# A token router: ranks by full comparison and one-hot products, against a threshold searched by its bits and rows moved by indirect DMA

## The chip, the cores and the metric

The kernel runs on one core of a Trainium2 chip. The core has a matrix engine (TensorE, PE in the profile; its weight loads are the row PEld), a vector engine (VectorE, DVE), an activation engine (ScalarE, ACT), a general engine (GpSimd, POOL) and a queue engine (SyncE, SP) that only issues DMAs here. Each engine works through its own list of instructions in order and waits on semaphores. The metric is device time in microseconds for one execution, the median over runs.

## The reference

One sequence of 2048 tokens with 128 features passes through two layers. Each layer computes `x + s * silu(f)`, where `s` is an attention of the normalised input and `f` a second branch.

- First layer, `s`: attention with 16 heads of 8 features over all 2048 tokens, with relu in place of softmax; then an output product and a layer norm.
- First layer, `f`: a block for a few tokens. A router gives each token a weight (`x @ router_w + b`). The 255 tokens with the greatest weights are fetched in order of their place in the sequence, pass through a causal softmax attention with rotary positions and a small feed-forward part, are multiplied by their weight, and are put back at their places. All tokens whose weight is not above the 256th greatest keep `x`:

```
topv, topi = jax.lax.top_k(weights, k)          # k = 256
thr = topv[:, -1]
sel_mask = (weights > thr[:, None])
sel_idx = jnp.sort(topi[:, :kc], axis=1)        # kc = 255
...
out = jnp.zeros_like(x).at[bidx, sel_idx].set(proc)
return out + x * (1.0 - sel_mask)[..., None]
```

- Second layer: causal softmax attention with 16 heads of 64 features and a gated feed-forward part.

The selection must be exact: which tokens are among the 255, the threshold, and the places.

## The kernel before

**The loop.** `relu_attention` (L680) holds the first layer's attention as a loop of 256 steps (L964), n = 16 * (4 * qc + g) + kb, over 4 blocks of 512 queries, 4 groups of 4 heads and 16 blocks of 128 keys. A step issues four score products (`scores`, L824) into banks of PSUM, four evictions with relu (on ACT, L832, or on DVE, L834), and the four products with the values of the step two before (`products`, L840). Score banks are six, evicted tiles twelve, so engines may run about a step apart. In some steps a projection for later keys or queries stands behind them (`all_keys`, `all_queries`: `spread`, L728 on PE, L733 on ACT, L734 on DVE, then DMAs L738); in all other steps one turn of a generator of side work (`next(other)`, L976).

**The side work.** `others` (L950) runs `routed_block` (L217), then loads weights of the second layer, then `gated` (L863) for each block of queries that is ready. A `yield` ends a turn, so a piece of side work that is written between two `yield`s falls into one step of the loop. PE, ACT and DVE run exactly in the order in which the program is written (`manual_schedule`, L88); the lists of SP and POOL are arranged by the framework. Which of ACT and DVE takes an eviction is decided by `Work.lesser` (L189): it holds a running sum of planned work for each, to which side work adds its own with `work.add`, and gives the eviction to the one with the lesser sum.

**The router before.** PE forms the weights of all tokens as a row repeated in all partitions (`wrow`, 128 x 2048, L281) and as columns (`wcol`, 128 x 16, L289). The rank of every token is then counted on DVE: for each of 16 blocks of 128 tokens one comparison with all earlier tokens (L303), one with all others (L310) and one inside the block that settles ties (L314). For each pair of blocks two one-hot matrices 128 x 256 (`hot`, L331: is the token's rank equal to the column's number) are multiplied on PE with the rows `xne` (131 columns: 128 features, weight, place, position; L341), and the results are summed in `xs` on DVE (L346). The 256th row gives the threshold through a product with a mask of the last row (`last`, L353). So the fetched rows stand in order of weight; the block's own causal mask is fetched by their places (`mcols`, L366, and `msel`, L417, the two indirect DMAs of this kernel, on POOL).

**The way back before** (L632 to L677). For each block of 512 tokens DVE makes two one-hot matrices 128 x 512 (`place`, L642), PE multiplies them with the block's result `proc` (L652, 8 products of 128 columns), DVE adds the tokens that keep `x` (`unsel`, L658), ACT applies silu, and POOL folds in the bias, gamma and beta (L663 to L674). The blocks follow each other two or three steps apart.

**Around it.** At the start POOL makes constants (`tok`, `before`, `last`, L245 to L257), and clears `qk` and `v` (L268, L270), while DVE normalises the first tokens (`normalised`, L764 to L787, with L776 and the short chain L779 to L783). SP loads keys and queries of later groups back from DRAM (`group`, L742) between the DMAs of the side work.

Of the kernel before, what the change touches and what calls it, by code (L numbers as in the profile page):

```python
# [11 lines left out]
F32 = mybir.dt.float32  # L12
F32R = mybir.dt.float32r
BF16 = mybir.dt.bfloat16
I32 = mybir.dt.int32
U32 = mybir.dt.uint32
AF = mybir.ActivationFunctionType
ALU = mybir.AluOpType
AX = mybir.AxisListType
# [3 lines left out]
P = 128  # L23
S = 2048
D = 128
NC = S // P
NQ = S // 512
# [3 lines left out]
KSEL = 256  # L31
KC = KSEL - 1
SM = 512
NP = 8
NHB = 3
NS = 6
NEG = -1.0e30
MAGIC = 1.5 * 2.0**23

# [177 lines left out]
def routed_block(  # L217
# [3 lines left out]
    nc = tc.nc  # L221
    scale = 1.0 / math.sqrt(HD0)
    KB = (P, KC - P)

    def bank(shape):
        return ps.tile(shape, F32, tag="x", name="x")
# [3 lines left out]
    for t, n in enumerate(("wq", "wk", "wv")):  # L230
# [10 lines left out]
    nc.sync.dma_start(out=pos, in_=a["pos"])  # L241


    tok = rb.tile([P, 512], F32, name="tok")
    nc.gpsimd.iota(  # L245
        tok, pattern=[[1, 512]], base=0, channel_multiplier=0,
        allow_small_or_imprecise_dtypes=True,
    )
    before = rb.tile([P, P], F32, name="before")
    nc.gpsimd.memset(before, 1.0)  # L250
    nc.gpsimd.affine_select(
        out=before, in_=before, pattern=[[-1, P]], compare_op=ALU.is_gt,
        fill=0.0, base=0, channel_multiplier=1,
    )
    last = rb.tile([P, P], F32, name="last")
    nc.gpsimd.memset(last, 1.0)
    nc.gpsimd.affine_select(  # L257
        out=last, in_=last, pattern=[[0, P]], compare_op=ALU.is_ge,
        fill=0.0, base=-(P - 1), channel_multiplier=1,
    )  # L260
    nc.gpsimd.iota(
        xne[:, :, 129], pattern=[[P, NC]], base=0, channel_multiplier=1,
        allow_small_or_imprecise_dtypes=True,
# [11 lines left out]
    wrow = rb.tile([P, S], F32, tag="wrow_qkT", name="wrow")  # L275
    wcol = rb.tile([P, NC], F32, name="wcol")
    for i in range(NQ + 1):
        if i < NQ:
            cols = slice(512 * i, 512 * i + 512)
            t = bank([P, 512])  # L280
# [4 lines left out]
        if i:  # L285
            t = bank([P, 4, P])
            for c4 in range(4):
                c = 4 * i - 4 + c4
# [3 lines left out]
            yield  # L292
    nc.gpsimd.tensor_copy(xne[:, :, 128], wcol)


    junk = rb.tile([P, S], BF16, tag="junk_mrows", name="junk")
    cnt = rb.tile([P, 3, NC], F32, name="cnt")
    nc.vector.memset(cnt, 0.0)
    for c in range(NC):
        w = wcol[:, c : c + 1]  # L300
        lo = c * P
        if c:
            nc.vector.tensor_scalar(  # L303
                junk[:, :lo], wrow[:, :lo], w, None, ALU.is_ge, ALU.add,
                accum_out=cnt[:, 0, c : c + 1],
            )
            if c >= NC // 2:
                work.add(d=0.2 + lo / 960)
                yield
        nc.vector.tensor_scalar(  # L310
            junk[:, lo:], wrow[:, lo:], w, None, ALU.is_gt, ALU.add,
            accum_out=cnt[:, 1, c : c + 1],
        )
        nc.vector.scalar_tensor_tensor(  # L314
            junk[:, :P], wrow[:, lo : lo + P], w, before, ALU.is_equal, ALU.mult,
            accum_out=cnt[:, 2, c : c + 1],
        )
        work.add(d=2.9 if c < NC // 2 else 2.7 - lo / 960)
        yield
    rank = rb.tile([P, NC], F32, name="rank")  # L320
    nc.vector.tensor_reduce(rank, cnt.rearrange("p a c -> p c a"), AX.X, ALU.add)


    xs = rb.tile([P, 2, 131], F32, name="xs")
    made = []
    for c in range(-2, NC, 2):
        hots = made
        if c + 2 < NC:
            made = [rw.tile([P, KSEL], F32, tag="og", bufs=4, name="hot") for _ in range(2)]
            for i in range(2):  # L330
                nc.vector.tensor_scalar(  # L331
                    made[i], tok[:, :KSEL], rank[:, c + 2 + i : c + 3 + i], None, ALU.is_equal
                )
            work.add(d=0.7)
        if c < 0:
            yield
            continue
        t = bank([P, 2, 131])
        for b in range(2):
            for i in range(2):  # L340
                nc.tensor.matmul(  # L341
                    t[:, b, :], hots[i][:, b * P : (b + 1) * P], xne[:, c + i, 0:131],
                    start=(i == 0), stop=(i == 1),
                )
        if c:
            nc.vector.tensor_tensor(xs, xs, t, ALU.add)  # L346
        else:
            nc.vector.tensor_copy(xs, t)
        work.add(d=0.5)
        yield  # L350
    thr = small.tile([P, 1], F32, tag="thr")
    t = bank([P, 1])
    nc.tensor.matmul(t, last, xs[:, 1, 128:129], start=True, stop=True)  # L353
    nc.vector.tensor_copy(thr, t)
    unsel = rb.tile([P, NC], F32, name="unsel")
    nc.vector.tensor_scalar(unsel, wcol, thr, None, ALU.is_le)

# [49 lines left out]
    for b in range(2):  # L407
        t = bank([P, 4, P])
# [113 lines left out]
    for g in range(G):  # L522
# [28 lines left out]
        prT = []  # L551
# [78 lines left out]


    b_out, gamma, beta, xin = rest  # L632
    at = small.tile([P, 2, NQ], F32, tag="at")
    for i in range(NQ):
        nc.gpsimd.tensor_scalar(at[:, :, i], xs[:, :, 129], 512.0 * i, None, ALU.subtract)
    for i in range(NQ + 1):
        if i:
            put = place
        if i < NQ:
            place = [rw.tile([P, 512], F32, tag="prT", bufs=4, name=f"place{b}") for b in range(2)]  # L640
            for b in range(2):
                nc.vector.tensor_scalar(place[b], tok, at[:, b, i : i + 1], None, ALU.is_equal)  # L642
            work.add(d=1.0)
            yield
        if not i:
            continue
        cs = slice(4 * i - 4, 4 * i)
        t = bank([P, 4, D])
        for c4 in range(4):
            for b in range(2):  # L650
                n = KB[b]
                nc.tensor.matmul(  # L652
                    t[:, c4, :], put[b][:n, c4 * P : (c4 + 1) * P], proc[:n, b, :],
                    start=(b == 0), stop=(b == 1),
                )
        for c4 in range(4):
            c = 4 * i - 4 + c4
            nc.vector.scalar_tensor_tensor(  # L658
                g0[:, c, :], xne[:, c, 0:D], unsel[:, c : c + 1], t[:, c4, :],
                ALU.mult, ALU.add,  # L660
            )
        work.add(d=1.4)
        nc.gpsimd.tensor_tensor(  # L663
            xne[:, cs, 0:D], xne[:, cs, 0:D], b_out.unsqueeze(1).to_broadcast([P, 4, D]), ALU.add
        )
        yield
        nc.scalar.activation(g0[:, cs, :], g0[:, cs, :], AF.Silu)
        work.add(a=0.7)
        u = rw.tile([P, 4, D], F32, tag="qkv", name="gb")
        nc.gpsimd.tensor_tensor(  # L670
            u, g0[:, cs, :], beta.unsqueeze(1).to_broadcast([P, 4, D]), ALU.mult
        )
        nc.gpsimd.tensor_tensor(xin[:, cs, :], xin[:, cs, :], u, ALU.add)
        nc.gpsimd.tensor_tensor(  # L674
            g0[:, cs, :], g0[:, cs, :], gamma.unsqueeze(1).to_broadcast([P, 4, D]), ALU.mult
        )
        yield  # L677


def relu_attention(  # L680
# [1045 lines left out]
```

## Time and profile before

| | |
|---|---|
| median of 3 runs | 1487.89 us (1487.07 to 1488.57) |
| the profiled execution: its time | 1487.12 us |
| the profiled execution: its span, first to last instruction | 1485.1 us |
| mean granted clock of TensorE | 0.991 |
| DMA | 44.70 MB, mean 30 GB/s |
| loop of the first layer, first scores to last products | 37.7 to about 505 us |

The page gives the busy time of each engine, then the span in 40 equal slices (37.1 us each) with the busy share of a slice in tenths. A group of instructions is told by line, engine, operation and tile. A matmul's end is modelled, so TensorE can look busy while it waits; the distance between the starts of like instructions is the safer measure. A matmul of two fp32 operands is recorded as two instructions.

### The profile page before, as it was taken

The page shows a single profiled execution, that of the slowest core. Times are in us where ns is not written, and L with a number is a line of the kernel's source. Part 1 is how long each engine was busy: PE and PEld are TensorE (multiplying, and loading weights), DVE is VectorE, ACT ScalarE, POOL GpSimd, SP SyncE. Part 2 cuts the span into 40 slices and gives each one's busy share as a digit, 9 for nine tenths or more (in the row PEclk, how much of TensorE's full clock was granted, in tenths as well). Part 3 has the DMA queues.
Part 4 walks back from the last instruction along what each step waited for, and adds up shares of the span by engine and source line. Part 5 has one row for each costly group of instructions (what it writes and reads, how often), then busy time and mean ns, then how long its engine had stood idle before and what let it go on. Part 6 is the DMA issues. An engine that isn't in the chain of part 4 may idle for free.

```text
span 1485.1 us, 27124 instructions
## 1 busy us (share of the span) xinstructions
PE 1431.8 (96%) x10336; PEld 877.3 (59%) x10336; DVE 1079.6 (73%) x1938; ACT 967.2 (65%) x2080; POOL 325.2 (22%) x445
## 2 busy tenths in 40 slices
PE   4999999999999999999999999999999999999997
PEld 2223233332222367777777777777777777777775
DVE  5797878778888667567677667667767766777765
ACT  2787878778878656656556556556656655665663
POOL 1001000050000123322332242242242232252310
PEclk8999999999999999999999999999999999999999
DMA  2621100100200220000010010010001001000000
GB/s 66 186 66 61 32 12 14 49 26 14 60 20 4 79 50 15 15 16 15 21 24 15 15 30 15 15 29 15 15 15 29 15 15 29 15 15 16 15 22 22
DMA packets 28192, 44.70 MB, mean 30 GB/s; under 512 B 5984, under 2 KB 14560, under 8 KB 28064
## 3 DMA queue, kind: packets, MB, share of 16 engines
q1 hardware_dynamic: 27376, 41.94, 11.0%
q8 instruction: 81, 1.33, 0.4%
q0 software_dynamic: 256, 0.79, 0.2%
q14 instruction: 47, 0.39, 0.1%
q10 hardware_dynamic: 432, 0.26, 0.1%
HBM read 14.76 MB, written 10.11 MB: 17 GB/s over the span
## 4 chain that ended last, share of the span: by engine, by line
PE 60%; ACT 2%; DVE 1%; issue 1%; DVEq 0%; ACTq 0%
PE t L1326 18%; PE z L1376 17%; PE t L1556 16%; PE m L1436 2%; PE m L1264 2%; PE m L1229 2%; PE m L1279 2%; PE m L1421 2%; ACT p L1360 1%; ACT pt L1563 1%; PE m L1158 0%; DVE tops L1347 0%; PE m L1176 0%; DVE t L1346 0%; DVE pt L1563 0%
## 5 line engine op out<-in xcount | busy, mean ns | idle before, releaser
L1347 DVE TENSOR_REDUCE tops<-t 128x1 f32<-128x1024 f32 (+4 forms) x320 | 334.6, 1062 | 63.2 <-PE t L1326 56.0
L832 ACT ACTIVATE rt<-t 128x512 f32<-128x512 f32 x620 | 326.3, 625 | 76.1 <-PE t L824 75.0
L1563 ACT COPY pt<-t 128x512 f32<-128x512 f32 (+3 forms) x359 | 163.4, 518 | 266.9 <-PE t L1556 265.8
L1360 ACT ACTIVATE p<-t,tops 128x1024 f32<-128x1024 f32 (+7 forms) x384 | 331.2, 882 | 2.9 <-DVE tops L1347 2.2
L1326 PE MATMUL t<-k,q 128*128 128x512 f32 (+4 forms) x1280 | 316.6, 390 | 7.4 <-ACT p L1360 7.4
L834 DVE TENSOR_SCALAR rt<-t 128x512 f32<-128x512 f32 x404 | 261.2, 684 | 45.4 <-PE t L824 38.6
L840 PE MATMUL t<-rt,va 128*9 128x512 f32 x2048 | 270.3, 601 | 4.2 <-ACT part L856 3.8
L1556 PE MATMUL t<-ident,p 128*128 128x128 f32 x2176 | 270.1, 275 | 3.0 <-ACT x L1250 1.4
L1376 PE MATMUL z<-pt,v 128*64 128x256 f32 (+1 forms) x2304 | 268.3, 374 | 0.5 <-ACT zs L1570 0.5
L1326 PEld LDWEIGHTS t<-k,q 128*128 128x128 f32 x1280 | 218.6, 189 | 79.7 <-issue 36.1
L1556 PEld LDWEIGHTS t<-ident,p 128*128 128x128 f32 x2176 | 244.0, 141 | 25.5 <-ACT pt L1563 2.9
L1376 PEld LDWEIGHTS z<-pt,v 128*64 128x64 f32 x2304 | 151.6, 136 | 86.9 <-issue 21.4
L824 PEld LDWEIGHTS t<-qT,kT 32*128 32x128 f32 x1024 | 64.8, 183 | 189.0 <-ACT rt L832 112.9
L1563 DVE COPY pt<-t 128x512 f32<-128x512 f32 (+3 forms) x289 | 163.5, 605 | 2.6 <-PE z L1376 1.5
L824 PE MATMUL t<-qT,kT 32*128 32x512 f32 x1024 | 157.3, 500 | 4.5 <-DVE rt L834 3.1
L1346 DVE TENSOR_TENSOR t<-t,mask_q 128x128 f32<-128x128 f32 (+1 forms) x192 | 65.0, 339 | 85.8 <-PE t L1326 78.3
L1252 POOL CAST q<-x 64x512 fp32r<-64x512 f32 x60 | 36.8, 613 | 371.7 <-ACT x L1250 338.9
L1360 ACT ACTIVATION_READ_ACCUMULATOR p<-t,tops 128x1 f32 x384 | 84.1, 219 | 0.0
L1426 DVE TENSOR_TENSOR zs<-zs,m 128x512 f32<-128x512 f32 (+1 forms) x49 | 32.7, 676 | 64.3 <-PE m L1421 64.1
L1254 POOL TENSOR_TENSOR k<-x,k 64x512 fp32r<-64x512 f32 x60 | 76.4, 1273 | 4.6
L1254 POOL TENSOR_TENSOR q<-x,q 64x512 fp32r<-64x512 f32 x60 | 76.3, 1272 | 4.6
L840 PEld LDWEIGHTS t<-rt,va 128*9 128x9 f32 x2048 | 30.7, 88 | 69.5 <-issue 61.0
(291 smaller groups left out, 1068.1 us busy)
## 6 DMA issues: line engine op xcount, KB each, us to landing
q<-q SPq DMA_DIRECT2D x64, 256.0 KB
spread<-high SPq DMA_DIRECT2D x16, 256.0 KB
spread<-low SPq DMA_DIRECT2D x16, 256.0 KB
qT<-spread SPq DMA_DIRECT2D x15, 256.0 KB
kT<-spread SPq DMA_DIRECT2D x12, 256.0 KB
xin<-in_x SPq DMA_DIRECT2D x4, 256.0 KB
on<-part SPq DMA_DIRECT2D x64, 16.0 KB
wide<-inverse SPq DMA_DIRECT2D x32, 32.0 KB
```

What stands on the lines that cost most here:

```text
L824: nc.tensor.matmul(t, kT[rows, g, kb * P : (kb + 1) * P], qTs[qc, g][rows, :], start=True, stop=True,)
L832: nc.scalar.activation(rt, t, AF.Relu, scale=scale)
L834: nc.vector.tensor_scalar(rt, t, scale, 0.0, ALU.mult, ALU.max)
L840: nc.tensor.matmul(acc[32 * j : 32 * j + HD0 + 1, :], va[:, kb, 4 * g + j, :], r[j], start=(kb == 0), stop=(kb == NC - 1),)
L1254: nc.gpsimd.tensor_tensor(low, x[half(e), :], high, ALU.subtract)
L1326: nc.tensor.matmul(flat[:, at_x : at_x + y - x], q[:, part, c4 * P : (c4 + 1) * P], k[:, x:y], start=(part == 0), stop=(part == 1),)
L1346: nc.vector.tensor_tensor(last, last, mask, ALU.add)
L1347: nc.vector.tensor_reduce(M[pr, c // 4][:, h, c % 4, es], x, axes, ALU.max, negate=True)
L1360: nc.scalar.activation(dst, x, AF.Exp, bias=M[pr, c // 4][:, h, c % 4, e : e + 1], accum_out=Z[pr, c // 4][:, h, c % 4, e : e + 1],)
L1376: nc.tensor.matmul(l1.z[half(e), slot, lo:2, :], V[pr, h][:, kb, half(e)], pts[e][:, kb, lo:2, :], start=(kb == 0), stop=(kb >= n0 - 1), s ...
L1556: nc.tensor.transpose(t[:, k + b, :], x[lo + b], ident)
L1563: copy(dst, t)
```

## The change

All of it is in `routed_block`; the loop, the rest of the block and the second layer are as before.

- **Threshold.** The 256th weight is found as a bit pattern. The sign comes from one count over `wcol`, summed over partitions by a product with ones. Then five rounds, with shifts 24, 17, 10, 3 and 0, each set 7 bits (3 in the last): every partition tries another value of the field, counts on DVE over `wrow` how many weights reach it (one pass over 2048 values), compares with 256, and a product with a mask of ones on PE counts in how many partitions that held, which is the field. A round takes two turns.
- **Slots.** Two flags per token (above, equal), prefix sums over the 16 blocks on DVE (five doubling steps) and over the partitions by two products on PE give each token its place among the selected. The fetched rows so stand in order of sequence, not of weight; rows equal to the threshold come behind.
- **Fetching.** Sixteen one-hot matrices 128 x 256 in bf16 (`hots`) are multiplied with two columns (block number and partition: `place`) for the token number of each slot. Two indirect DMAs on POOL fetch the rows of `xs` from a table `rows` in DRAM, which SP has written from `xne` as soon as the weights stood. Five turns pass before the rows are used.
- **The way back.** A table `back` in DRAM is cleared at the start (four DMAs of SP from a cleared tile). Two indirect DMAs on POOL write `proc` into it (unused rows go to a row 2048), four DMAs of SP read it back (`came`), twelve turns pass, and then the four blocks of 512 tokens follow each other five turns apart instead of two or three. The one-hot matrices and their products are gone.
- **Constants.** POOL makes `ones`, `number`, `fields`, `outside`, `place` and the cleared tile in place of `before` and `last`.

The diff at its core:

```diff
+SHIFTS = (24, 17, 10, 3, 0)
...
+    back = dram.tile([S + 1, D], F32, tag="back", bufs=1, name="back")
+    nothing = rw.tile([P, 4, D], F32, tag="prT", bufs=4, name="nothing")
+    nc.gpsimd.memset(nothing, 0.0)
+    for i in range(NQ):
+        nc.sync.dma_start(
+            out=back[512 * i : 512 * i + 512, :].rearrange("(c p) d -> p c d", p=P), in_=nothing
+        )
...
+    rows = dram.tile([S, 131], F32, tag="rows", bufs=1, name="rows")
+    nc.sync.dma_start(out=rows.rearrange("(c p) d -> p c d", p=P), in_=xne[:, :, 0:131])
...
-    for c in range(NC):
-        w = wcol[:, c : c + 1]
-        lo = c * P
...
+    for i in range(len(SHIFTS)):
+        nc.vector.tensor_tensor(tried, bits, fields[:, i : i + 1], ALU.bitwise_xor)
+        nc.vector.tensor_scalar(
+            junk, wrow, tried.bitcast(F32), None, ALU.is_ge, ALU.add, accum_out=cnt
+        )
+        nc.vector.tensor_scalar(enough, cnt, float(KSEL), None, ALU.is_ge)
+        work.add(d=2.9)
+        yield
+        yield
+        t = bank([P, 1])
+        nc.tensor.matmul(
+            t, ones[:, 2 if i == len(SHIFTS) - 1 else 1, :], enough, start=True, stop=True
+        )
+        nc.vector.tensor_scalar(found, t, float(2 ** SHIFTS[i]), None, ALU.mult)
+        nc.vector.tensor_tensor(bits, bits, found, ALU.bitwise_xor)
...
+    for i in range(5):
+        x, y, n = sums[i % 2], sums[1 - i % 2], 1 << i
+        nc.vector.tensor_copy(y[:, :n], x[:, :n])
+        nc.vector.tensor_tensor(y[:, n:], x[:, n:], x[:, : 2 * NC - n], ALU.add)
+    work.add(d=3.0)
+    yield
+    yield
...
     for c in range(NC):
+        nc.vector.tensor_scalar(hots[:, c, :], tok, slot[:, c : c + 1], None, ALU.is_equal)
+        work.add(d=0.35)
+        if c % 4 == 3:
+            yield
...
+    for b in range(2):
+        t = bank([P, 2])
+        for c in range(NC):
+            nc.tensor.matmul(
+                t, hots[:, c, b * P : (b + 1) * P], place[:, c, :],
+                start=(c == 0), stop=(c == NC - 1),
+            )
...
+        nc.gpsimd.indirect_dma_start(
+            out=xs[:, b, :], out_offset=None, in_=rows[:, :],
+            in_offset=bass.IndirectOffsetOnAxis(ap=token[:, b : b + 1], axis=0),
+        )
+        yield
...
+    for _ in range(5):
+        yield
...
+    for b in range(2):
+        nc.gpsimd.indirect_dma_start(
+            out=back[:, :], out_offset=bass.IndirectOffsetOnAxis(ap=home[:, b : b + 1], axis=0),
+            in_=proc[:, b, :], in_offset=None,
+        )
+    came = []
     for i in range(NQ):
...
+        t = rw.tile([P, 4, D], F32, tag="prT", bufs=4, name="came")
+        nc.sync.dma_start(
+            out=t, in_=back[512 * i : 512 * i + 512, :].rearrange("(c p) d -> p c d", p=P)
+        )
+        came.append(t)
+    for _ in range(12):
+        yield
...
-                nc.tensor.matmul(
-                    t[:, c4, :], put[b][:n, c4 * P : (c4 + 1) * P], proc[:n, b, :],
-                    start=(b == 0), stop=(b == 1),
-                )
...
-        yield
+        for _ in range(4):
+            yield
```

## The prediction

> **What bounds the kernel now.** I read the page first, then the busy time of each engine in 20 us windows, then the timeline inside the stages that the change touches. On the page TensorE (PE) is busy nearly throughout; VectorE (DVE) and ScalarE (ACT) are near full only in slices 2 to 4.
>
> ```profile
> PE 1431.8 (96%) x10336; PEld 877.3 (59%) x10336; DVE 1079.6 (73%) x1938; ACT 967.2 (65%) x2080; POOL 325.2 (22%) x445
> PE   4999999999999999999999999999999999999997
> DVE  5797878778888667567677667667767766777765
> ACT  2787878778878656656556556556656655665663
> ```
>
> A busy PE can be a waiting PE, so the stages matter. Busy time by window (PE, PEld, DVE, ACT, POOL, granted clock, DMA share, GB/s):
>
> ```profile
> 60.00:80.00 20.00, 19.52 (x140) 5.19 (x136) 19.16 (x41) 18.59 (x38) 0.21 (x1) 1.00 0.80 248
> 80.00:100.00 20.00, 17.67 (x108) 4.43 (x100) 19.86 (x42) 15.66 (x32) 0.00 (x0) 0.83 0.14 43
> 100.00:120.00 20.00, 19.18 (x144) 5.94 (x142) 19.81 (x46) 18.19 (x37) 0.00 (x0) 1.00 0.03 5
> 120.00:140.00 20.00, 20.00 (x158) 9.47 (x157) 12.18 (x28) 12.61 (x25) 0.86 (x4) 1.00 0.21 67
> 480.00:500.00 20.00, 19.73 (x172) 4.28 (x168) 17.34 (x27) 15.91 (x31) 0.00 (x0) 1.00 0.03 6
> ```
>
> From 60 to 120 us, while the ranks are counted, DVE is full (19.2 to 19.9 of 20). From 120 to 140 PE is full and DVE 61%. At 480 to 500, with no side work, PE sets the pace. How long a step of the loop takes is the distance between two quartets of scores (L824). A step without side work, then a step with the one-hot products (L341), then one with the way back (L652), from the timeline:
>
> ```profile
> 61.64 0.51 PE L824 MATMUL t<-qT,kT 32*128 32x512 f32 x4
> 62.08 1.05 PE L840 MATMUL t<-rt,va 128*9 128x512 f32 x8
> 63.05 0.51 PE L824 MATMUL t<-qT,kT 32*128 32x512 f32 x4
> ...
> 117.00 1.16 PE L341 MATMUL x<-xne,hot 128*128 128x131 f32 x8
> 118.09 0.51 PE L824 MATMUL t<-qT,kT 32*128 32x512 f32 x4
> ...
> 301.97 2.05 PE L652 MATMUL x<-proc,place 128*128 128x128 f32 x16
> 303.95 0.51 PE L824 MATMUL t<-qT,kT 32*128 32x512 f32 x4
> ```
>
> So a clean step is 1.41 us (61.64 to 63.05), L341 adds 1.09 (117.00 to 118.09), L652 adds 1.98. Work that PE gets in a step of such a stage goes straight onto the end time. The layer after (from 505 us) is not touched; the loop must run its 256 steps whatever the router does.
>
> **The change part by part.** The sum is made against the profiled execution, 1487.12 us (span 1485.1 and 2.0 around it), 0.8 under the median 1487.89.
>
> **Counting.** Before, from step 11 (61.64) to step 38 (start 115.35), 27 steps (108 scores L824) take 53.7 us; which work stands in which step comes from the order of the two built programs. Their PE work is 27 x 1.41 and two projections L728 at 1.06 (as 47.06 to 48.12): 40.2. The excess is 13.5. The trace says why: DVE has 43.5 us of counting there (52.9 busy less 9.4 of evictions L834), and ACT takes nearly all evictions back to back at 0.5 us each:
>
> ```profile
> 75.66 15.68 ACT L832 ACTIVATE rt<-t 128x512 f32<-128x512 f32 x31
> 77.65 1.81 DVE L310 TENSOR_SCALAR_CACHE_REDUCE junk<-wrow,wcol 128x1536 bf16<-128x1536 f32 x1
> ```
>
> After, the same stage ends at step 37. A round is: matmul of 1 column, found, bits, tried, one count over 2048, enough. DVE cost: the count 2.35 (row of L310 at 128x2048), 0.08 to read its sum, four small ones at the 0.2 us spacing of L780 to L783: 3.2. The order of the built program gives DVE 1 to 2 evictions a round (1.7, at 0.64 = 1.1) and ACT 6 or so (3.0), so a round of two steps is 4.3 and DVE-bound; five rounds with the eviction of one projection (0.7) 22.2, where PE needs 10 x 1.41 + 1.06 = 15.2: excess 7.0. Steps 25 and 26 hold 16 small DVE ops (found, bits, want, the prefix sums) at 0.2 = 3.2 and an eviction: 4.2 against 2.8, excess 1.4. Steps 27 to 30 make slots (0.8) and 16 one-hots in bf16. No row has bf16 in and out; two fp32 ones of the same size take 0.60 to 0.62 (0.30 each), a small op 0.16, so 16 cost 2.6 to 4.8; I take 4.0, since the fixed part is the larger. With 16 evictions shared this is 6.6 against 5.64: excess 1.0. The first round's start adds 0.5. Excess after: 9.9.
>
> PE work changed: away 8 x L341 = 8.7 and L353 (a step of 1.73, so 0.3). New: eight small matmuls (new L358, L371, L394, L397), hidden because DVE and not PE sets those steps (if that cover is gone, at most 0.3 each as L353, 2.4); and 32 single-pass products of 2 columns with 128-column loads (new L422), in steps 30 and 31, not hidden. Bounds per pair: above, an L341 pair, 1.09/8 = 0.136; below, a load L840 of 9 columns, 0.015 (eight in 0.12). So 0.5 to 4.4; I take 3.0, near the upper row because the loaded width is the same.
>
> The clock: the page of windows has 0.83 for 80 to 100, three steps of 2.5 to 2.8 us, part of the 13.5. PE idles a little more in the new rounds (2.9 of 4.3), so the same loss is likely; I add 1.0 for half a chance of about 2. The Trainium skill (TensorE: Matmul & The Clock Gate, Part 1) has a rule that speaks against the change: an idle window of about 3.4 us halves the clock until a busy one. By that rule alone no round, with gaps of 1.4 us, would halve it; here it halved with gaps under 1 us a step, so the measured loss stands and the sum by the rule would be 1.0 lower.
>
> Counting stage: -8.7 - 0.3 - 13.5 + 9.9 + 3.0 + 1.0 = -8.6.
>
> **Fetching rows.** The zero writes of back stand on SP between r_pos (10.45 us) and the first spread (41.85): hidden by that gap of 31 us, and nothing waits behind them. The table of 1.07 MB goes out on SP ahead of two kT loads (L742); the trace moves up to 256 GB/s at 50 to 80 us, so it holds them about 4 us. kT of step 20 was issued at 63.87 for a use at 78.5: hidden, and 11 us would have to go first. The gather is issued by POOL in steps 30 and 31; DVE waits for it in step 37 (new L448) with the evictions of 37 and 38 behind it, and PE behind those. Rows of mcols landed 4.1 us after issue; token, POOL's 1.1 to 1.2 per issue twice and 4.1 make about 7 of the 8.5 us to step 37. I take 0.2; if the cover goes, each us late costs one.
>
> **The nine turns saved** (the first transposes of hn move from step 52 to 43) are no gain by themselves: nine later steps now run clean at 1.41.
>
> **Way back.** Steps 128 to 142 took 31.7 (296.94 to 328.69) against 15 x 1.41 = 21.2: excess 10.6, of which L652 is 4 x 1.98 = 7.9 and the rest late place (L642, 0.43 each in pairs) and L658 behind it. After, L642 and L652 are gone; L658, in steps 131 to 147 five apart, leaves about 0.4 each: 1.6. New: two scatters on POOL, behind proc (1.21 for two), landing some 7.5 us after the last product; SP's four loads wait for that and then take about 5.5 (as xin at the start, issued from 0.80). 13 us of the 17 that 12 turns give: hidden. Behind them on SP stand qT for step 160 and group outputs of step 129: not urgent. If the cover goes, one for one. Gain 9.0.
>
> **Start.** POOL gets about 2.2 us more: two memsets 128x512 (0.5 each, half of L268's 0.94), selects (0.29 for 128 columns) and small ones, less what goes. DVE opens the kernel, and it was held up while POOL's memsets ran:
>
> ```profile
> 7.95 0.94 POOL L268 MEMSET qk<- 128x1024 f32 x1
> 8.58 1.46 DVE L776 TENSOR_SCALAR ln_v<-ln_mv 128x4 f32<-128x4 f32 x1
> 8.84 0.94 POOL L270 MEMSET r_v<- 128x1024 f32 x1
> 13.65 0.17 DVE L776 TENSOR_SCALAR ln_v<-ln_mv 128x4 f32<-128x4 f32 x1
> ```
>
> The same op took 1.46 beside them and 0.17 later. With more small POOL work DVE may get in between earlier (-1.3) or wait to POOL's end (+2.2); I take +0.8. The Trainium skill (SBUF — State Buffer, Who interferes with whom) gives the reason: the two share a port pair, the second to come blocks until the first ends. By that rule, with POOL never free, the sum would be 1.4 higher.
>
> **Sum.** 1487.1 - 8.6 + 0.2 - 9.0 + 0.8 = 1470.5.
>
> **Rivals.**
> (a) A cover goes: the gathered rows or the scattered ones land late. For it: new L448 has only some 1.5 us to spare, and 2048 rows of 524 bytes are a size no row shows. Against: 4.1 and 3.5 us for both older gathers. With 8 to 12 us of lateness 1478 to 1483.
> (b) PE stays on half clock (the side where it is slower). For it: the halving at 91 to 98 us came in just such a stage. A step then takes 2.55. Ten round steps lose 0.4 each, every other one 1.1: to pass 1491 it needs some 15 steps beyond the rounds, 38 us more. Against: at half clock PE is full, and the trace had its clock back after 7 us. 1491 to 1500.
> (c) The rounds cost more than PE saves: PE, DVE and ACT take turns, a round becomes 3.2 + 3.0 = 6.2, five cost 9.5 more: 1480.
> (d) No gain to measure (within 0.2%, 3 us, about what a measurement of this kernel tells apart): a late scatter gives all back, 1485 to 1490.
>
> **How the numbers follow.** The forecast has 0.68, its own range 1464 to 1477: down 6.5 for bf16 one-hots (1.4), L422 (2.5), start (2.1) and clock (0.5), up 6.5 for L422 (1.4), start (1.4), small matmuls (2.4) and clock (1.3). (a) 0.12, (c) 0.08, (b) 0.06, (d) 0.03, and 0.03 below 1464. Leaving out two in ten gives 1462 to 1481. Faster 0.91, same 0.03, slower 0.06.
>
> **What would show it.** Right: DVE no longer full from 66 to 110 us, rounds of about 4.3 us, L422 steps near 2.9, no step of 3.5 around the way back, the loop's end 16 to 17 us earlier, the second layer equal. Wrong: idle DVE before new L448, PE behind the came loads, the first scores later than 39 us, or a clock under 0.9 beyond 110 us.

## The result, and the profile after

The kernel after takes 1470.62 us (median of 4 runs, 1469.37 to 1472.82) against 1487.48 for the kernel before (4 runs): a ratio of 0.9888, 95% interval 0.9875 to 0.9900. The profiled execution took 1469.37 us, with a span of 1467.7 us and a mean granted clock of 0.993. The forecast was 1470.5. The number is right; what follows shows that its terms are not.

The page of after, busy time and two rows of the 40 slices:

```profile
PE 1412.9 (96%) x10254; PEld 864.2 (59%) x10254; DVE 1061.1 (72%) x1911; ACT 955.0 (65%) x2053; POOL 330.5 (23%) x457
DVE  5788888787888486577677677667767767777765
ACT  2688877788887467666556556556556656656553
```

PE has 18.9 us less to do than before. DVE no longer stands at the top of its scale in any slice. By window (columns as for before: PE, PEld, DVE, ACT, POOL, granted clock, DMA share, GB/s):

```profile
60.00:80.00 20.00, 18.82 (x138) 5.79 (x134) 16.42 (x32) 15.47 (x31) 0.21 (x1) 1.00 0.96 263
80.00:100.00 20.00, 18.68 (x158) 6.21 (x150) 18.03 (x62) 17.65 (x35) 0.00 (x0) 1.00 0.24 70
100.00:120.00 20.00, 19.56 (x170) 4.82 (x170) 16.30 (x36) 15.47 (x34) 5.02 (x9) 1.00 0.25 72
```

In the counting stage DVE has 16.3 to 18.0 of 20 us where before it had 19.2 to 19.9, and the clock stays at 1.00 (0.83 before in 80 to 100). Two rounds on DVE, from the timeline:

```profile
81.76 0.15 DVE L374 TENSOR_SCALAR found<-x 128x1 int32<-128x1 f32 x1
...
82.40 2.35 DVE L363 TENSOR_SCALAR_CACHE_REDUCE junk<-wrow,tried 128x2048 bf16<-128x2048 f32 x1
...
84.86 0.68 DVE L917 TENSOR_SCALAR rt<-t 128x512 f32<-128x512 f32 x1
85.46 0.15 DVE L374 TENSOR_SCALAR found<-x 128x1 int32<-128x1 f32 x1
...
86.10 2.35 DVE L363 TENSOR_SCALAR_CACHE_REDUCE junk<-wrow,tried 128x2048 bf16<-128x2048 f32 x1
...
88.56 1.28 DVE L917 TENSOR_SCALAR rt<-t 128x512 f32<-128x512 f32 x2
89.75 0.15 DVE L374 TENSOR_SCALAR found<-x 128x1 int32<-128x1 f32 x1
```

From `found` to `found` a round takes 3.70 us with one eviction on DVE and 4.29 with two. The products that give the token numbers:

```profile
97.73 0.57 PE L907 MATMUL t<-qT,kT 32*128 32x512 f32 x4
...
99.21 0.55 PE L422 MATMUL x<-place,hots 128*128 128x2 bf16 x16
99.69 0.51 PE L907 MATMUL t<-qT,kT 32*128 32x512 f32 x4
```

Sixteen of them cost 0.55 us: this step took 1.96.

**Where the time went.** For each kernel I take the start of each of the 256 quartets of scores and subtract 1.414 us a step; what is left is the excess, which can be compared between kernels whose side work stands in other steps. All figures are from the profiled executions, in us. "Router" runs from the first scores to the first transposes of hn, "block" to the step of the product that gives `proc`, "way back" to four steps past the last block's adds, "rest" to the last scores, "turn" from there to the second layer's first scores, "layer 2" to the end. A row's numbers and 360.6 (255 steps of 1.414) add up to its span.

| kernel | first scores | router | block | way back | rest | turn | layer 2 | span |
|---|---|---|---|---|---|---|---|---|
| before | 37.7 | 34.7 | 43.5 | 10.5 | 13.9 | 31.4 | 952.7 | 1485.1 |
| after | 36.9 | 21.5 | 42.2 | 3.7 | 15.7 | 34.2 | 952.9 | 1467.7 |
| router_only | 37.4 | 21.5 | 42.2 | 9.5 | 14.4 | 31.2 | 954.1 | 1470.7 |
| wayback_only | 38.2 | 34.9 | 45.0 | 3.3 | 17.8 | 31.3 | 954.3 | 1485.2 |
| back_close | 37.9 | 21.5 | 42.2 | 12.1 | 16.4 | 32.6 | 952.9 | 1476.1 |
| even_and_order | 38.3 | 21.0 | 42.4 | 3.4 | 13.8 | 30.0 | 952.8 | 1462.3 |

After against before: -0.8, -13.2, -1.3, -6.9, +1.8, +2.8, +0.1. The router gains half as much again as forecast, and two parts that the diff does not touch give 4.6 us back. The block's 1.3 lies where before stood at half clock for 3.41 us (from 183.8) and after did not: from 18 to 21 steps behind the first transposes of hn before lost 4.8 us, after 3.0.

The two losses can be read in the trace. At the end of a group of heads ACT copies the finished group (L939), and PE waits for the copy, because the next products go into the same bank:

```profile
460.03 1.58 ACT L915 ACTIVATE rt<-t 128x512 f32<-128x512 f32 x3 [0.33 <-PE t L907]
461.48 0.60 ACT L939 COPY part<-t 128x512 f32<-128x512 f32 x1
462.14 1.05 PE L923 MATMUL t<-rt,va 128*9 128x512 f32 x8 [0.73 <-ACT part L939]
```

Three evictions stand ahead of the copy on ACT. In before there were two at the like place, and PE waited 0.27 us:

```profile
481.37 1.09 ACT L832 ACTIVATE rt<-t 128x512 f32<-128x512 f32 x2 [0.31 <-PE t L824]
483.00 1.05 PE L840 MATMUL t<-rt,va 128*9 128x512 f32 x8 [0.27 <-ACT part L856]
```

Which engine takes an eviction comes from the running sums of planned work, and the new router and way back have moved these sums. The turn to the second layer:

```profile
493.43 1.02 PE L1277 MATMUL m<-xn1T,f_w_gate 128*128 128x512 f32 x2
494.64 1.38 ACT L1326 ACTIVATE k<-m,b_k 64x512 fp32r<-64x512 f32 x2 [4.81 <-DMA b_k<-in_b_K]
496.70 2.03 PE L1278 MATMUL m<-xn1T,f_w_up 128*128 128x512 f32 x2 [2.25 <-ACT g L1291]
498.52 1.85 PE L1277 MATMUL m<-xn1T,f_w_gate 128*128 128x512 f32 x2
```

ACT waits for a bias of a few KB, PE behind it idles 2.25 us (1.15 in before), and the products after that take 1.85 to 2.03 instead of 1.02: the clock is at half for 3.41 us.

### The profile page after: what moved, and what is told of

The parts are those of the page before. It is cut to its first block, busy times and chain, and to the rows that moved or that the text cites. A ratio compares the mean times of both kernels' runs of the same rounds, so it can differ in the third digit from the quotient of the medians.

```text
span 1467.7 us, 26963 instructions
## 1 busy us (share of the span) xinstructions
PE 1412.9 (96%) x10254; PEld 864.2 (59%) x10254; DVE 1061.1 (72%) x1911; ACT 955.0 (65%) x2053; POOL 330.5 (23%) x457
## 4 chain that ended last, share of the span: by engine, by line
PE 61%; ACT 2%; DVE 1%; issue 1%; DVEq 0%; ACTq 0%
PE t L1409 18%; PE z L1459 17%; PE t L1639 16%; PE m L1519 2%; PE m L1347 2%; PE m L1312 2%; PE m L1362 2%; PE m L1504 2%; ACT p L1443 1%; ACT pt L1646 1%; PE m L1241 0%; DVE tops L1430 0%; PE m L1259 0%; DVE t L1429 0%; DVE pt L1646 0%
## 5 line engine op out<-in xcount | busy, mean ns | idle before, releaser
L915 ACT ACTIVATE rt<-t 128x512 f32<-128x512 f32 x595 | 314.4, 604 | 69.5 <-PE t L907 68.3
L917 DVE TENSOR_SCALAR rt<-t 128x512 f32<-128x512 f32 x429 | 277.2, 684 | 52.5 <-PE t L907 48.1
L923 PE MATMUL t<-rt,va 128*9 128x512 f32 x2048 | 267.3, 595 | 5.6 <-ACT part L939 5.6
L907 PE MATMUL t<-qT,kT 32*128 32x512 f32 x1024 | 153.0, 496 | 1.5 <-ACT rt L915 1.1
L1335 POOL CAST k<-x 64x512 fp32r<-64x512 f32 x60 | 36.6, 611 | 158.3 <-ACT x L1333 156.6
```

The source lines that it names most:

```text
L907: nc.tensor.matmul(t, kT[rows, g, kb * P : (kb + 1) * P], qTs[qc, g][rows, :], start=True, stop=True,)
L915: nc.scalar.activation(rt, t, AF.Relu, scale=scale)
L917: nc.vector.tensor_scalar(rt, t, scale, 0.0, ALU.mult, ALU.max)
L923: nc.tensor.matmul(acc[32 * j : 32 * j + HD0 + 1, :], va[:, kb, 4 * g + j, :], r[j], start=(kb == 0), stop=(kb == NC - 1),)
L1335: nc.gpsimd.tensor_copy(high, x[half(e), :])
```

## Experiments

### The two halves of the change: router_only and wayback_only

router_only is after with before's way back. Its core:

```diff
-    for b in range(2):
-        nc.gpsimd.indirect_dma_start(
-            out=back[:, :], out_offset=bass.IndirectOffsetOnAxis(ap=home[:, b : b + 1], axis=0),
-            in_=proc[:, b, :], in_offset=None,
-        )
...
+            for b in range(2):
+                nc.vector.tensor_scalar(place[b], tok512, at[:, b, i : i + 1], None, ALU.is_equal)
```

> The new router with the old way back (one-hot matrices 'place' and their products). Computes the same as both kernels. Theory A, from the comparison of the two traces: the router's part of the loop is worth 13.2 us (time over 1.41 us a step: 34.7 us up to the first transposes of hn before, 21.5 after), the start 0.8, so 1487.5 - 14 = 1473.5 with up to 4 us given back later: 1472 to 1478, and PE time over 1.41 us a step near 21 up to the transposes and near 10.5 around the way back. Theory B, the sums of the prediction: counting and fetching -8.4, start +0.8, so 1479 to 1481.

Measured: 1471.54 us (4 runs, 1471.19 to 1472.42) against 1487.22; ratio 0.9892, interval 0.9876 to 0.9909. The excess of the router is 21.5, as in after, and the way back's 9.5. Theory A held by its place and size (the time lies 0.5 below its 1472 to 1478, since nothing was given back later); theory B's 1479 to 1481 fell.

wayback_only is before with after's way back, each row sent home by its own place:

```diff
+    home = rb.tile([P, 2], U32, name="home")
+    nc.vector.tensor_tensor(outside, outside, xs[:, :, 129], ALU.max)
+    nc.vector.tensor_copy(home, outside)
```

> The old router with the new way back (scatter to DRAM, four loads, blocks five turns apart); the fetched rows stand in order of weight and go home by their own places. Computes the same as both kernels. Theory A (traces): the way back is worth 7.7 us, 1479 to 1481, with the time over 1.41 us a step around it falling from 11.1 to about 3.4. Theory B (prediction): 9.0 us, 1477 to 1479. Rival: the parts do not add, the way back gains only where the router left room; then this kernel stays within 3 us of 1487.5. If the parts add, the two gains of this kernel and of the one with the new router alone sum to 16 to 18 us.

Measured: 1487.13 us (10 runs, 1483.15 to 1489.92) against 1487.22; ratio 0.9995, interval 0.9985 to 1.0006. Both theories fell, and the rival's time came out. Locally the gain is there: the way back's excess falls from 10.5 to 3.3. But 3.9 us come back in the rest of the loop, 1.5 in the block and 1.6 in the second layer. The greatest single piece is at one step:

```profile
412.25 1.05 PE L852 MATMUL t<-rt,va 128*9 128x512 f32 x8
414.11 1.26 POOL L889 TENSOR_TENSOR on<-on,wide 128x512 f32<-128x512 f32 x1 [15.70 <-DMA wide<-inverse]
415.42 1.41 PE L897 MATMUL t<-w_out,on 128*128 128x128 f32 x8 [2.13 <-POOL on L889]
416.20:419.60 3.40, 3.40 (x20) 1.04 (x18) 2.12 (x6) 1.57 (x3) 0.00 (x0) 0.50 0.00 0
```

The output product of a finished block of queries (L897) waits for DMAs that had come late. The side work now stands 15 to 21 turns later, so the block's `inverse` (issued at 405.7) came behind the five DMAs of a group that finished just then (402.3 to 405.6 on SP). A half-clock stretch follows, and steps 201 and 202 take 4.7 us over 1.414 each; the like product cost 1.1 to 1.3 in before. In time the two alone, 15.7 and 0.1, come to 15.8, against 16.9 together; what did not come out is a way back worth 9 us.

### Is a round set by DVE: half_counts and double_counts

half_counts counts over 1024 of the 2048 weights, so it finds another threshold and fetches other tokens; the rest of its work is of the same size. double_counts makes each count twice.

```diff
         nc.vector.tensor_scalar(
-            junk, wrow, tried.bitcast(F32), None, ALU.is_ge, ALU.add, accum_out=cnt
+            junk[:, :1024], wrow[:, :1024], tried.bitcast(F32), None, ALU.is_ge, ALU.add, accum_out=cnt
         )
```

> After, but each of the five rounds counts over the first 1024 weights instead of 2048, so another threshold is found and other tokens are fetched; all other work is of the same size. If DVE sets the rounds (the prediction: 3.2 us of DVE for the round and 1.1 for evictions, 4.3 us per two steps), each round falls by about 1.2 us to 3.1, in all -5 to -6 us in steps 13 to 25. If PE, ACT and DVE take turns or ACT sets them, the rounds fall by less than 0.6 each, in all -1 to -3 us.

> After, but each round's count over 2048 weights is made twice (2.35 us more of DVE a round); computes the same. If DVE sets the rounds: 5 x 2.35 = +11.8 us in steps 13 to 25. If it has slack beside PE and ACT: +4 to +8. If a TensorE that waits more falls to half clock, as in the counting of before (6.8 us at half clock there, none in after): more than +14 and a granted clock under 0.9 between 70 and 105 us.

Measured, one run each: 1465.48 and 1483.93 us. A count over 1024 takes 1.28 us instead of 2.35, so 5.4 us left DVE, but the router's excess fell by 2.4 only (21.5 to 19.1), 0.5 a round: the rival held. Doubling put 11.8 us onto DVE and 12.7 onto the path (34.2). So the rounds of after sit at the knee: below about 3.4 us a round (83.76 to 87.19 in half_counts) evictions and PE's own 2.83 set the pace, above it every us of DVE is paid. The clock theory of double_counts was half right:

```profile
60.00:80.00 20.00, 16.84 (x108) 4.72 (x100) 16.99 (x30) 12.74 (x25) 0.21 (x1) 0.91 0.91 249
80.00:100.00 20.00, 13.85 (x86) 3.55 (x86) 19.30 (x29) 11.18 (x22) 0.00 (x0) 0.83 0.30 92
```

With PE at 13.85 of 20 us the clock does fall, in four stretches of 3.41 us. If all of the 11.8 us was paid, it cost the 0.9 us between 12.7 and 11.8.

### The covers: fetch_early and back_early

fetch_early leaves out the five turns ahead of the fetched rows' first use; back_early waits 2 turns instead of 12 for the rows on the way back (`range(12)` becomes `range(2)`). The edit of fetch_early:

```diff
     nc.vector.tensor_copy(home, outside)
-    for _ in range(5):
-        yield
```

> After, without the five turns between the gather of the rows and their first use (L448 in step 32 instead of 37, about 103 us instead of 110.9). In after the second gather is issued at 102.5 and lands some 2.6 us behind its issue. Theory: the five turns cover the gather with about 5 us to spare; without them DVE waits 2 to 4 us at L448 and the loop loses 1 to 3 us. Rival (a) of the prediction in its strong form, a gather that takes 8 us or more: the loop loses 5 us or more. Rival, the turns are not needed: nothing is lost.

> After, with 2 turns instead of 12 between the scatter and the first block of the way back. In after the scatters are issued at 270.9 and 274.1, SP's loads at 278.4 to 280.4, the first use is at 288.7. Theory: about 5 us of the 17 are to spare, so 14 us less of cover make DVE wait 7 to 10 us at the first block, and the loop loses 6 to 8.5 us there. Rival: evicted tiles and banks in hand cover most of it, the loop loses under 4 us.

Measured, one run each: 1469.02 and 1473.94 us. The first waits of DVE in each:

```profile
105.15 0.17 DVE L446 TENSOR_SCALAR clamped<-xs 128x2 f32<-128x2 f32 x1 [1.64 <-DMA xs<-rows,token]
```

```profile
281.02 1.14 DVE L740 SCALAR_TENSOR_TENSOR g<-xne,unsel,came 128x128 f32<-128x128 f32 x4 [5.00 <-DMA came<-back]
```

The gathered rows were there at 105.1, and in after they are used at 110.9: 5.8 us to spare. DVE waited 1.6 us in fetch_early, less than the theory's 2 to 4, and the excess up to the transposes of hn is 21.6, as in after: the tiles in hand cover that much. In back_early the loads let DVE go at 281.0, 7.7 us before after's first use (288.7); DVE waited 5.0, one step lost 5.8 us, and the way back as a whole 4.3 (excess 8.0 against 3.7). That lies between the theory's 6 to 8.5 and the rival's 4: cover and tiles in hand were both a little more than the theory had. Rival (a) of the prediction, late rows, is so answered: 5.8 and 7.7 us were in hand.

### The distance of the blocks: back_close

```diff
-        for _ in range(4):
-            yield
+        yield
```

> After, with the four blocks of the way back two turns apart instead of five. In after the steps 131 to 148 take 2.3 us over 1.41 a step. Theory: the old way back was slow by its products on PE (4 x 2 us) and by 'place' on DVE ahead of the adds; without these the distance of the blocks matters little, +0 to +1 us. Rival: the spacing itself is a good part of the gain, +2 to +4 us.

Measured: 1477.80 us (one run). The way back's excess is 12.1 against 3.7: the theory fell, and the loss is more than twice what the rival gave. The timeline of back_close says why; the adds of the second and the third block, and POOL beside the third:

```profile
292.49 1.13 DVE L740 SCALAR_TENSOR_TENSOR g<-xne,unsel,came 128x128 f32<-128x128 f32 x4
...
296.06 1.28 POOL L756 TENSOR_TENSOR g<-g,row_gamma 128x512 f32<-128x512 f32 x1
296.51 4.90 DVE L740 SCALAR_TENSOR_TENSOR g<-xne,unsel,came 128x128 f32<-128x128 f32 x4
297.30 1.33 POOL L745 TENSOR_TENSOR xne<-xne,row_b_out 128x512 f32<-128x512 f32 x1
298.59 1.33 POOL L752 TENSOR_TENSOR gb<-g,row_beta 128x512 f32<-128x512 f32 x1
300.00 1.26 POOL L755 TENSOR_TENSOR xin<-xin,gb 128x512 f32<-128x512 f32 x1
```

Four adds that take 1.13 us when POOL is idle take 4.90 and, in the last block, 4.70 while POOL works through its four operations of a block back to back. That is 7.3 of the 8.4 us lost; PE ran dry behind it and stood at half clock for 6.83 us from 308.2, which is in the loss too. In before the adds of the second block ran beside the same POOL work at 1.12 us; what was held up there was `place` (0.87 in the other three blocks):

```profile
309.92 1.27 POOL L673 TENSOR_TENSOR xin<-xin,gb 128x512 f32<-128x512 f32 x1
310.72 1.12 DVE L658 SCALAR_TENSOR_TENSOR g<-xne,unsel,x 128x128 f32<-128x128 f32 x4 [1.55 <-PE x L652]
311.15 1.28 POOL L674 TENSOR_TENSOR g<-g,row_gamma 128x512 f32<-128x512 f32 x1
...
313.76 2.85 DVE L642 TENSOR_SCALAR place<-tok,at 128x512 f32<-128x512 f32 x2
```

The difference is the second operand. L658 read PE's result in PSUM (`x`); L740 reads the rows that DMA brought into SBUF (`came`). The Trainium skill (SBUF — State Buffer, Who interferes with whom) states just this: a DVE instruction with two SBUF inputs contends with a GpSimd instruction that reads SBUF. So the five turns are not a refinement of the new way back: two turns apart it has 12.1 us of excess, more than the 10.5 of the old one. Five steps last at least 7.1 us, and POOL's four operations 5.1.

### The losses that the diff does not name: bias_first, part_even, zeros_first, all_three

bias_first issues the second layer's two biases ahead of its three weights. part_even deals the evictions of the step in which a group ends ACT, DVE, ACT, DVE. zeros_first makes POOL's large clears before its copies of the weights. all_three has all of them.

```diff
-        for n in ("W_K", "W_Q", "W_V"):
-            W[n] = lw.tile([P, NP * P], F32, name=f"w_{n}")
-            nc.sync.dma_start(out=W[n], in_=a[n])
         l1.b_q = lw.tile([P, NP], F32, name="b_q")
         nc.sync.dma_start(out=l1.b_q, in_=a["b_Q"])
         l1.b_k = lw.tile([P, NP], F32, name="b_k")
         nc.sync.dma_start(out=l1.b_k, in_=a["b_K"])
+        for n in ("W_K", "W_Q", "W_V"):
+            W[n] = lw.tile([P, NP * P], F32, name=f"w_{n}")
+            nc.sync.dma_start(out=W[n], in_=a[n])
```

```diff
-        for rt, t in r:
-            if work.lesser(512):
+        for j, (rt, t) in enumerate(r):
+            if n >= 2 and (n - 2) % 16 == 15:
+                first = j % 2 == 0
+                work.add(a=0.6 * first, d=0.68 * (1 - first))
+            else:
+                first = work.lesser(512)
+            if first:
```

> After, with the two biases of the second layer's queries and keys (2 small DMAs) issued on SP ahead of the three weights instead of behind them; nothing else changes. In after ACT waits 4.8 us for b_k behind the loop (489.8 to 494.6), PE then idles 2.25 us and runs 3.4 us at half clock; from the last scores (480.6) to the first scores of the second layer (514.8) pass 34.2 us, against 31.4 before. Theory: the wait and the half clock behind it cost 2.8 to 4.5 us there; with the biases early that stretch takes 30 to 31.5 us and the kernel 1466 to 1468. Rival: the stretch is set by PE and by the weights w_W_K themselves, and stays at 33 to 34.5 us.

> After, with the evictions of the step in which a group of heads ends dealt out evenly, ACT DVE ACT DVE, instead of by the running sums of planned work. In after a third eviction on ACT (1.57 us) stands ahead of ACT's copy of the finished group (L939) in most group ends, and PE waits for that copy: steps 162 to 242 take 0.72, 0.60, 0.79, 0.40, 0.73 and 0.80 us over 1.41; before, with two, 0.34 in most. Theory: these steps fall to about 0.35 each, 1.9 us less from step 162 on and 2 to 3 us less in all. Rival: the lost time moves to the next step, since the same evictions are made in all: within 0.5 us of after.

> After, with POOL's five large clears (nothing, qk, r_v, ones) made in POOL's idle 1.4 to 4.3 us, ahead of the copies of the weights, instead of at 7.8 to 13.2 us. If DVE's small operations of the first normalisation (L859 to L868) are held up by POOL's long operations, as in before (1.46 us for an operation of 0.17) and less in after (0.43 to 0.63, and 1.67 against 1.11), the first scores come 0.3 to 1.3 us earlier than 36.9. If the hold-up comes from POOL being busy at all, they move by less than 0.3 or come later, since the copies now run where the clears ran.

> After with the three changes together: biases first, even evictions at the group ends, clears first. If they add: -3.5 (biases) -2.5 (group ends) -0.5 (start) = 1464 us, within 1462 to 1467. If a part shows nothing by itself, the sum is smaller by that part.

| | median of runs (lowest, highest) | ratio to before, 95% interval |
|---|---|---|
| bias_first | 1468.82 (1468.46, 1472.69) | 0.9877 (0.9859 to 0.9895) |
| part_even | 1470.31 (1468.24, 1471.41) | 0.9873 (0.9857 to 0.9890) |
| zeros_first | 1470.29 (1467.17, 1472.22) | 0.9879 (0.9858 to 0.9899) |
| all_three | 1467.41 (1466.08, 1470.69) | 0.9866 (0.9849 to 0.9883) |

Each alone has an interval that overlaps that of after (0.9875 to 0.9900), so the readings rest on the traces, one of each. part_even did what it was made for: the seven group ends from step 146 on cost 0.34 each (after: 0.34 to 0.80), and the rest of the loop 13.8 instead of 15.7. Its own run then lost 3 us in the block, where PE stood at half clock for 6.83 us from 156.1. bias_first missed: the stretch stayed at 33.8 us, as its rival had it. The wait moved. With two small DMAs ahead of it, w_W_K came to stand behind the finished group's five DMAs on SP (4.2 us later, counted from the last scores), and PE waited 1.92 us at the product that reads it. That it waited for w_W_K is inferred: the profile names `sums` on DVE, which ended last but is no operand of that product. A half-clock stretch of 3.41 us followed, as in after. zeros_first took DVE's hold-ups at the start away (no operation of the normalisation over 0.41 us, up to 1.08 in after), and the fourth group of tokens began 1.5 us earlier on DVE (19.08 against 20.58). Yet the first scores came at 36.9, as in after: PE's half clock at the start lasted to 34.0 us there, to 32.6 in after. all_three's 1467.4 lies above its range of 1462 to 1467. In its trace the loop's excess is 2.5 below that of after, as forecast for the group ends, and the turn takes 31.7 us: PE again waited at the first product with w_W_K, 1.44 us, but no half clock followed. The start gave nothing, and the second layer took 1.6 more than in after.

### The order that follows: even_and_order

Even evictions as above, and the biases between the weights; `zeros_first` is left out.

```diff
...
             W[n] = lw.tile([P, NP * P], F32, name=f"w_{n}")
             nc.sync.dma_start(out=W[n], in_=a[n])
-        l1.b_q = lw.tile([P, NP], F32, name="b_q")
-        nc.sync.dma_start(out=l1.b_q, in_=a["b_Q"])
-        l1.b_k = lw.tile([P, NP], F32, name="b_k")
-        nc.sync.dma_start(out=l1.b_k, in_=a["b_K"])
+            if n == "W_K":
+                l1.b_k = lw.tile([P, NP], F32, name="b_k")
+                nc.sync.dma_start(out=l1.b_k, in_=a["b_K"])
+                l1.b_q = lw.tile([P, NP], F32, name="b_q")
+                nc.sync.dma_start(out=l1.b_q, in_=a["b_Q"])
```

> After with even evictions at the group ends and the loads of the second layer in the order w_W_K, b_k, b_q, w_W_Q, w_W_V. With the biases ahead of all weights, the wait moved to w_W_K (PE idle 1.9 and 1.4 us there), since the finished group's five DMAs then stood between; in this order w_W_K keeps its place ahead of them and b_k comes 1.4 us earlier than in after, with no large weight ahead of it in flight but w_W_K. Theory: ACT no longer waits for b_k, PE's idle of 2.25 us at 14 us behind the last scores falls under 0.9, no half clock follows, the stretch from the last scores to the first scores of the second layer takes 30.5 to 31.5 us against 34.2, and the loop is 2 to 2.7 us shorter by the group ends: 1465 to 1467.5. Rival: b_k lands as late as before because latency and not the queue sets it: the stretch stays at 32 to 34.

Measured: 1464.03 us (5 runs, 1463.63 to 1464.13) against 1487.51; ratio 0.9839, interval 0.9825 to 0.9852. This is below the interval of after, and 1 us below the theory's 1465 to 1467.5. The two lines that answer to those of after:

```profile
489.87 1.38 ACT L1332 ACTIVATE k<-m,b_k 64x512 fp32r<-64x512 f32 x2 [1.12 <-PE m L1318]
492.35 1.02 PE L1283 MATMUL m<-xn1T,f_w_gate 128*128 128x512 f32 x2
493.21 1.02 PE L1284 MATMUL m<-xn1T,f_w_up 128*128 128x512 f32 x2
```

ACT waits for PE, as it should, not for the bias; PE has no gap there and no product at half clock. The turn takes 30.0 us against 34.2, and the loop's excess falls by 2.5 us. So both losses were real, and the two changes together are worth 6.6 us of median. The 34.2 of after is at the upper end of its kind: in the seven other kernels with its order of loads the turn took 32.1 to 34.3 us, about 1.7 more where the half clock came. The order was not tried without the even evictions.

## Why the prediction was right, and where it was not

By its own steps, against the profiled executions:

- **The old counting stage, -13.5, and its products, -9.0.** Held: steps 11 to 38 show 13.4 without the projections, steps 38 to 52 show 9.7. One reading was wrong: the "three steps of 2.5 to 2.8 us" at half clock are two, one of 5.37 us and one of 2.55. The first score of step 26 started at 90.22, the other three at 93.03, behind an eviction that stood behind counts on DVE:

```profile
90.22 0.49 PE L824 MATMUL t<-qT,kT 32*128 32x512 f32 x1
93.03 0.79 PE L824 MATMUL t<-qT,kT 32*128 32x512 f32 x3 [2.33 <-DVE rt L834]
```

- **The new excess, +9.9: too great.** Steps 11 to 31 of after show 7.9 without L422. The rounds made 5.4 to 5.9, by where one begins to count, and not 7.0. Their time was right: from the first `bits` (67.23) to the last `found` (89.75) DVE took 22.5 us where 22.2 was forecast, four rounds at 3.7 to 4.3 and the one with the projection at 6.1. What failed is PE's share, "10 x 1.41 + 1.06 = 15.2". The step with the projection holds no turn, so the five rounds lie in eleven steps (13 to 23), and PE needs 16.6 there. half_counts adds that DVE is only just the bound. The sixteen small operations came every 0.1 to 0.2 us, and four one-hots took 0.86, not 1.0.
- **L422, +3.0: the worst-sized term of the stage, 1.0 measured.** "Near the upper row because the loaded width is the same" took the row of fp32 operands with 131 columns as the nearest; two bf16 operands with 2 columns came out at 0.55 per sixteen, 0.034 each, nearer to the lower bound.
- **The clock, +1.0: nothing.** No half clock in the counting of after. double_counts shows that the danger was real and, there, cheap. The reading "here it halved with gaps under 1 us a step" was off: the half clock of before began at 91.65, inside the gap of 2.33 us above. That it came without an idle window stands, since PE was busy for 72% of the 3.41 us ahead of it.
- **Fetching, +0.2:** covered by 5.8 us; the rows landed 2.5 to 2.7 us behind each issue, not 4.1. Together the stage gave 13.2 where 8.4 was forecast, and by itself, in router_only, 15.7 us of time. Rival (c), rounds in turns, did not happen; half_counts shows that its idea, engines other than DVE in the round, holds for shorter counts.
- **The way back, -9.0: this step failed.** The old excess was sized right (10.6 forecast, 10.5 shown), and the cover held. But "L658 ... leaves about 0.4 each: 1.6" was 2.3 over steps 131 to 148 and 3.7 with the turns ahead of them, and above all the gain was booked as time. Alone it changed the time by -0.1 us, with an interval from -2.2 to +0.9; on top of the router it brought 0.9 between two medians whose intervals overlap. What came in its place: a later position of all that follows, which met other work (the `wide` DMAs in wayback_only, the group ends in after, the bias load). Of the old stage's rest, `place` was held up in one block of four (2.85 us instead of 0.87); the adds took 1.1 us in each and waited for PE.
- **The start, +0.8: not settled.** It read -0.8. But nine kernels with the same start as after had their first scores anywhere from 36.5 to 38.3 us, so no term of this size can be read from one execution.
- **"The second layer equal"** held (952.7 and 952.9), but the turn in front of it, which no term had, lost 2.8.

So the router gained 4.8 more than forecast, the start 1.6 and the block 1.3; the way back gained 2.1 less, and 4.6 were lost where no loss was foreseen. These cancel but for about 1 us. That the number came out so close is luck, not sizing; that the router pays, and that DVE sets its rounds, was right. Two of the signs named beforehand failed in the same way: the steps with L422 took 1.9 to 2.0 us and not 2.9, and the last scores came 20.4 us earlier and not 16 to 17, of which the turn then gave 2.8 back.

## What to carry to other kernels

When side work is moved to other turns, list what stands at the new places on each queue (the group's five DMAs, the copy behind the evictions, a small bias behind large weights): a local gain of 7 us was worth nothing measurable where these collided. When a one-hot product is replaced by a DMA into SBUF, look at who reads the result beside whom: the reader lost the PSUM operand that had kept it clear of POOL. And test a local gain alone, in time, before adding it to another.

## What the runs showed of the hardware

- **The half clock comes on a grid.** In all fourteen profiled executions the half-clock stretches last a multiple of 3.413 us (3.41, 6.83, 10.24, 13.65), but for the last one of each, which runs on past the last instruction, and within one execution those between 40 and 1440 us start a whole multiple of it apart. I cut each trace from 45 to 1400 us into this grid and added up PE's busy time in each piece. All 19 pieces at full clock with PE busy under 0.41 were followed by a half-clock piece; of the some 300 between 0.43 and 0.9 another 14 were. The two pieces of after around the bias:

```profile
493.40:496.80 3.40, 1.15 (x5) 0.33 (x3) 0.74 (x1) 2.12 (x4) 2.51 (x2) 1.00 0.90 264
496.80:500.20 3.40, 3.40 (x4) 1.35 (x5) 1.44 (x2) 0.33 (x1) 0.00 (x0) 0.50 0.08 22
```

  PE had 1.15 of 3.40 us, then half clock. half_counts had nearly the same gap, 2.10 us, but it fell across a border of the grid (1.71 of 3.40 busy), and its clock stayed at 1.00. So whether a gap of some 2 us costs 1.7 more depends on where it falls on the grid; it did in three of the eight kernels with this wait. The Trainium skill (TensorE: Matmul & The Clock Gate, Part 1) has the free-running window of 3413 ns; the runs agree on that, but not on an idle window as the condition, since a third of the window busy did not prevent it.
- **A bias of a few KB lands later in every kernel that has both halves of the change:** PE's gap there is 1.9 to 2.6 us in eight of them with after's order of loads, 0.9 to 1.2 in before, router_only and wayback_only, at the same distance of issue from the loop's end. The cause was not found.
- **The second layer** took 952.7 to 953.1 us in nine executions and 954.1 to 954.5 in five, which include two that changed only the first layer's router or way back. In four of the five the clock differs: part_even and all_three have their half-clock stretch 29.5 us behind the layer's first scores instead of 16 to 18 and lose 1.5 in the first 64 of its 1280 score products, router_only and zeros_first have a second stretch 934 us behind them. wayback_only has no such stretch and lost its 1.0 in the same 64; why was not tried.
